# Grouped convolutions in blocks of 2 by 2 pixels instead of 4 rows by 1, values in DRAM row by row, projection out in strips of 16 rows

## The chip, the cores and the metric

The kernel runs on one core of one Trainium2 chip. The time is that of the device for one execution, in microseconds (us). A core has five engines with a queue each: PE (TensorE) multiplies matrices, and loads the stationary operand of each product first (PEld in the profile); DVE (VectorE), ACT (ScalarE) and POOL (GpSimd) work on rows of elements; SP (SyncE) issues transfers (DMAs) in order, as ACT's queue also does here. All numbers are f32.

## The reference

Two layers over `x` of 4 images, 512 channels, 64 by 64 pixels. The first is a linear attention with a second, convolved set of heads:

```python
q = h @ wq.T; k = h @ wk.T; v = h @ wv.T            # h: x with channels last
qkv = concat([q, k, v])                             # 1536 channels
dw = conv(qkv, dw_kernel, groups=3*512)             # 5 by 5, 'SAME', each channel alone
pw = conv(dw, pw_kernel, groups=3*64)               # 1 by 1, in groups of 8 channels
f = concat([qkv, pw]).reshape(B, 128, 24, N)        # 128 heads of 8, N = 4096 pixels
query, key_ = relu(f[:, :, :8]), relu(f[:, :, 8:16])
value_pad = concat([f[:, :, 16:], ones])
scores = einsum('bhdn,bhen->bhde', value_pad, key_)
out = einsum('bhde,bhen->bhdn', scores, query)
out = out[:, :, :-1] / (out[:, :, -1:] + 1e-15)
x = bn(conv1x1(out, proj_kernel)) + x
```

The second layer takes four edge maps of each channel (`sobel`, `lap`, `diag`, `grad`, from 3 by 3 neighbourhoods), multiplies each with its own 128 by 512 matrix, applies gelu, scales the channels by an attention over image means, multiplies with a 512 by 512 matrix, normalises over channels, applies gelu and adds its input.

## The kernel before

**Groups.** The outer loop runs over 16 groups: 4 images `b` times 4 groups `g` of 128 channels for each of key, value and query. A group has two phases, written out by hand as lists of steps in the order in which PE runs them: `keys_and_values` (lines 563 to 591), which also carries the rest of the group before, and `queries` (593 to 616). PE's order is that of the program text; the other engines' instructions are placed by a scheduler.

**Strips.** An image lies in 8 strips of 512 pixels, `STRIPS`: a half of the image and a number `k`. Strip `k` of a half holds every fourth row of it, 8 rows of 64 pixels. `project` (262) makes a strip of key or query with 4 products (L268). ACT copies it, and its queue writes it into `inps` with 4 DMAs (L283), where the partitions hold 4 rows of 8 channels. `values` (285) makes a strip of values with pixels in partitions: its stationary operand is `x`, 128 pixels lying side by side, its moving operand the weight (16 products of 128 columns, L290). The result `vt` goes to DRAM (`near_dram`) with 4 DMAs (L303). `turn` (313) transposes a strip of keys with 4 products whose stationary operand is the strip (L316), and `scores` (322) multiplies keys and values.

**Convolved heads.** `convolve` (394) makes 5 by 5 and 1 by 1 convolution of keys or queries in one: a block is 4 rows of 1 pixel, 32 partitions hold 4 pixels of 8 channels, and 5 column shifts times 2 blocks of rows give 10 products, each on 16 tiles of 32 by 32 of the PE array (160 products a call, L402). A call makes half an image; there are 4 calls a group, 64 in all. For values the convolution comes after the sum over pixels: `correlate` (447) multiplies the convolved keys with values of the 8 rows by 5 columns around each block, 128 by 32 stationary and 160 columns moving (L457), from patches `near` that `load_near` (434) reads back from DRAM with 4 DMAs each into 3 buffers (`VALS`). `weigh` (469) multiplies the sums with the table `wtab` of kernel weights on DVE and reduces them (L475, L476).

**Behind.** The three later stages of an image, `project_out` (618), `edge_branches` (673) and `fuse_out`, are generators whose steps run between the steps of the next image's groups (`advance`, with costs and waits in a table). `project_out` makes an output strip for 4 parts of the channels: 8 products of 512 columns from `hd` tiles (4 from `heads`, 4 from `cheads`, L643 and L645, 11 buffers), then one DVE instruction that adds a shift and `x` (L666), then a DMA into `y` (L670). `edge_branches` reads windows of rows of `y` again.

**The last image** has nothing to run behind. Its `project_out` first runs 16 of its 32 steps, which is the upper half of the image; after that its edges start, 8 rows at a time, with further steps of `project_out` and of the third image's `fuse_out` between them (`fill`):

```python
for n in range(NCH * NJ // 2):
    next(projected)
    if n in (4, 8, 12):
        next(behind[0])
```

Of the kernel before, what the change touches and what calls it, by code (L numbers as in the profile page):

```python
# [15 lines left out]
P = 128  # L16
NCH = C // P
NG = 4
# [26 lines left out]


NB = H // 4 + 1
# [5 lines left out]
DXS = (0, -2, -1, 1, 2)  # L53
VROW = 4 * 66
# [19 lines left out]
FILL_EACH = (16 * FILL_Y + 40 * FILL_F - FILL_FIRST - FILL_ATT) / (4 * NJ // 2 - 1)  # L74
# [3 lines left out]
T_PROJ, T_TURN, T_SCORES, T_CONV, T_CORR, T_SMALL = 3.4, 0.5, 0.3, 10.6, 1.1, 0.9  # L78
# [11 lines left out]
def conv_seq_kernel(  # L90
# [27 lines left out]
    def squares(ap):  # L118

        return ap.rearrange("p (b x n) -> p n x b", b=4, n=4)  # L120
# [25 lines left out]
    for t in (KEY, QUERY):  # L146
        inps[t] = keep.tile([P, 4, NB, W], F32, name=f"inp{t}")
        nc.gpsimd.memset(inps[t][:, :, 0, :], 0.0)
        nc.gpsimd.memset(inps[t][:, :, NB - 1, :], 0.0)

# [5 lines left out]

    near = [dram.tile([2, NB, W + 4, 4, 66], F32, name=f"near{n}", bufs=1) for n in range(2)]

    mixed = dram.tile([NG, P, C], F32, name="mixed", bufs=1)

    def near_border(v):

        zeros = vals.tile([P, 8 * VROW], F32, name="zeros", tag="vals")
        nc.gpsimd.memset(zeros, 0.0)
        cols = v.rearrange("a b x r d -> (a b) x (r d)")
        for at in (0, W + 2):
            nc.sync.dma_start(out=cols[:, at : at + 2, :], in_=zeros[0 : 2 * NB, 0 : 2 * VROW])
        for b, r in ((0, 0), (NB - 1, 2)):
            nc.sync.dma_start(
                out=v[:, b, :, r : r + 2, :].rearrange("a x r d -> x a (r d)"),  # L170
                in_=zeros[0 : W + 4, 0:264],
            )
# [53 lines left out]
    class Group:  # L226
# [15 lines left out]
        def load_mat(self, t):  # L242

            dp = gw.tile([P, 4, 48], F32, name="dp_sb", tag="dp_sb", bufs=2)
            nc.sync.dma_start(out=dp, in_=dpk[self.g, t // QUERY])
            self.mat[t] = gw.tile([P, 4, 40, 8], F32, name="mat", tag="mat")
            nc.gpsimd.tensor_tensor(  # L247
                self.mat[t],
                dp[:, :, 0:40].unsqueeze(3).to_broadcast([P, 4, 40, 8]),
                dp[:, :, 40:48].unsqueeze(2).to_broadcast([P, 4, 40, 8]),  # L250
# [11 lines left out]
        def project(self, t, j):  # L262
# [12 lines left out]

            r, b = (k + 2) % 4, 8 * half + (k + 2) // 4
# [5 lines left out]
            for n in range(4):  # L282
                nc.scalar.dma_start(out=inps[t][r::4, n, b : b + 8, :], in_=rows(s)[32 * n : 32 * n + 32, :, :])  # L283

        def values(self, j):
            half, k = STRIPS[j]
            ps = ps_tile("val")
            for c in range(4):
                for n in range(NCH):
                    nc.tensor.matmul(  # L290
                        ps[:, ts(c, P)], lhsT=xs[self.b, j][n][:, ts(c, P)], rhs=self.w[VALUE][:, n, :],
# [8 lines left out]
            b = 8 * half + (k + 2) // 4  # L300
            for a in range(2):
                for jp in range(2):
# [820 lines left out]
```

## Time and profile before

| | us |
|---|---|
| median of 3 runs | 5008.83 |
| lowest and highest | 4993.76, 5010.05 |
| the profiled execution's own time | 5007.84 |
| its span, first to last instruction | 5006.1 |
| busy in L268 (`project`), PE | 955.0 |
| busy in L661 (`project_out`), PE | 905.8 |
| busy in L850 (`fuse_out`), PE | 468.8 |
| busy in L738 (`edge_branches`), PE | 468.9 |
| busy in L316 (`turn`), PE | 84.3 |

The profile was taken of one execution, so sums of its parts are made against 5007.84 us. Busy time of an engine is the time in which at least one instruction of it runs; durations of single PE instructions overlap, so their mean says less than the distance of their starts. A line of a group reads: line, engine, operation, output and inputs (moving operand first, then the stationary one), shape, number, then busy time and the mean of one in ns, then the idle time ahead of it and what ended most of it. Mean granted TensorE clock is 0.972 of full speed. The 16 DMA engines are busy with queue q1 (SP) in 52.7% and with q10 (ACT) in 6.4% of the span; 627939 packets moved 864.04 MB.

### The profile page before, as it was taken

Reading aid. Unit: us, or ns where it says so; the run is one execution under the profiler, and the core shown is the slowest. Engines: PE = TensorE matmul, PEld = TensorE weight load, DVE = VectorE, ACT = ScalarE, POOL = GpSimd, SP = SyncE. Lnnn points to the kernel's source line nnn. Section 1 sums busy time; section 2 is a strip of 40 time slices with the busy share of each in tenths; the row PEclk is TensorE's granted clock in tenths of the full one; section 3 lists DMA queues with packets and bytes.
Section 4 is the critical chain, followed back from the end, with each engine's and each line's share of the span. In section 5 each row is a group of like instructions: output and inputs, shape, how many; then the busy total and the mean of one; then the engine's idle time right before and its main releaser. Section 6 shows DMA issues by size and latency. Waiting matters only on the chain. (4 is left out here: it accounts for less than half of the span.)

```text
span 5006.1 us, 106244 instructions
## 1 busy us (share of the span) xinstructions
PE 4682.3 (94%) x46140; PEld 2687.1 (54%) x46140; DVE 2099.5 (42%) x2788; ACT 1580.6 (32%) x2713; POOL 369.7 (7%) x271
## 2 busy tenths in 40 slices
PE   9999999999999999799899999989998899899897
PEld 5665654455666654354465656444446565444343
DVE  1222222114565624311356553441125565537966
ACT  2112111003454523300244443430013444304675
POOL 0000000000000012200000000220000000000343
PEclk9999999999999999899999999999999999999998
DMA  6444467675666666676556656648666565475545
GB/s 192 137 127 133 139 192 195 156 162 167 189 194 187 187 189 195 194 180 164 149 187 188 189 183 201 187 159 225 155 161 187 168 183 163 140 171 144 165 153 169
DMA packets 627939, 864.04 MB, mean 173 GB/s; under 512 B 324072, under 2 KB 381448, under 8 KB 609040
## 3 DMA queue, kind: packets, MB, share of 16 engines
q1 hardware_dynamic: 548880, 756.51, 52.7%
q10 hardware_dynamic: 78592, 100.74, 6.4%
q8 instruction: 362, 5.93, 0.5%
q14 instruction: 105, 0.86, 0.1%
HBM read 575.93 MB, written 213.98 MB: 158 GB/s over the span
## 5 line engine op out<-in xcount | busy, mean ns | idle before, releaser
L268 PE MATMUL proj<-xt,w_sb 128*128 128x512 f32 x2048 | 955.0, 610 | 55.3 <-DMA xt<-in_x 33.4
L661 PE MATMUL yps<-hd,fold_sb 128*128 128x512 f32 x2048 | 905.8, 599 | 19.5 <-DMA hd<-heads 17.4
L402 PE MATMUL cv<-inp,mat 32*32 32x512 f32 x20480 | 731.9, 597 | 40.3 <-issue 33.1
L268 PEld LDWEIGHTS proj<-xt,w_sb 128*128 128x128 f32 x2048 | 382.5, 194 | 525.5 <-issue 450.5
L661 PEld LDWEIGHTS yps<-hd,fold_sb 128*128 128x128 f32 x2048 | 386.1, 191 | 510.1 <-issue 458.2
L402 PEld LDWEIGHTS cv<-inp,mat 32*32 32x32 f32 x20480 | 422.1, 103 | 318.8 <-issue 158.2
L850 PE MATMUL zps<-ef,wf_sb 128*128 128x512 f32 (+1 forms) x1056 | 468.8, 597 | 56.5 <-DMA ef<-ef 19.0
L290 PEld LDWEIGHTS val<-w_sb,xt 128*128 128x128 f32 x4096 | 471.2, 193 | 34.5 <-issue 27.5
L290 PE MATMUL val<-w_sb,xt 128*128 128x128 f32 x4096 | 485.8, 277 | 0.6 <-DVE z L857 0.4
L738 PE MATMUL br<-maps,wbr_sb 128*128 128x256 f32 (+1 forms) x1792 | 468.9, 415 | 3.7 <-DVE s_sb L335 2.9
L666 DVE SCALAR_TENSOR_TENSOR yt<-yps,shift,xr 128x512 f32<-128x512 f32 x128 | 96.0, 750 | 837.5 <-PE yps L661 784.0
L274 ACT COPY strip<-proj 128x512 f32<-128x512 f32 x256 | 149.1, 582 | 931.0 <-PE proj L268 908.0
L738 PEld LDWEIGHTS br<-maps,wbr_sb 128*128 128x128 f32 x1792 | 338.1, 192 | 142.9 <-issue 97.1
L457 PE MATMUL corr<-near,ckt 128*32 128x160 f32 x8192 | 333.6, 315 | 35.9 <-DMA near<-near 27.5
L850 PEld LDWEIGHTS zps<-ef,wf_sb 128*128 128x128 f32 x1056 | 203.4, 196 | 299.7 <-issue 229.1
L247 POOL TENSOR_TENSOR mat<-dp_sb 128x1280 f32<-128x1280 f32 x32 | 77.5, 2421 | 3486.4 <-PE cv L402 2856.8
L457 PEld LDWEIGHTS corr<-near,ckt 128*32 128x32 f32 x8192 | 256.5, 111 | 131.9 <-issue 72.1
L714 DVE TENSOR_TENSOR maps<-dv 128x1054 f32<-128x1054 f32 (+1 forms) x112 | 158.8, 1418 | 376.5 <-PE br L738 376.3
L318 ACT ACTIVATE kt<-tr 128x512 f32<-128x512 f32 x128 | 75.8, 592 | 532.4 <-PE tr L316 350.8
L366 DVE RECIPROCAL rec<-rec 128x512 f32<-128x512 f32 x64 | 214.4, 3350 | 1.7
L746 ACT ACTIVATE ef_o<-br,shift,scale 128x256 f32<-128x256 f32 (+1 forms) x224 | 131.2, 590 | 226.8 <-PE br L738 202.8
L881 POOL TENSOR_TENSOR z<-z,yr 128x512 f32<-128x512 f32 (+1 forms) x132 | 175.9, 1351 | 293.5 <-ACT z L878 172.5
(128 smaller groups left out, 3951.8 us busy)
## 6 DMA issues: line engine op xcount, KB each, us to landing
xt<-in_x SPq DMA_DIRECT2D x316, 512.0 KB
near<-near SPq DMA_DIRECT2D x512, 264.0 KB
inp<-strip ACTq DMA_DIRECT2D x1024, 64.0 KB
win<-y SPq DMA_DIRECT2D x96, 396.0 KB
near<-vt SPq DMA_DIRECT2D x512, 66.0 KB
y<-yt SPq DMA_DIRECT2D x128, 264.0 KB
heads<-q SPq DMA_DIRECT2D x128, 256.0 KB
cheads<-cq SPq DMA_DIRECT2D x128, 256.0 KB
```

The source lines that it names most:

```text
L268: nc.tensor.matmul(ps, lhsT=self.w[t][:, c, :], rhs=xs[self.b, j][c], start=(c == 0), stop=(c == NCH - 1))
L274: nc.scalar.copy(s, ps)
L290: nc.tensor.matmul(ps[:, ts(c, P)], lhsT=xs[self.b, j][n][:, ts(c, P)], rhs=self.w[VALUE][:, n, :], start=(n == 0), stop=(n == NCH - 1),)
L366: nc.vector.reciprocal(rec, rec)
L402: nc.tensor.matmul(rows(banks[i])[32 * j : 32 * j + 32, :, c0:c1], lhsT=self.mat[t][q, j, (dx + 2) * 8 + 4 * b : (dx + 2) * 8 + 4 * b + 4, :],
L457: nc.tensor.matmul(self.banks[jj][32 * i : 32 * i + 32, 160 * b : 160 * b + 160], lhsT=self.held["c", i][:, at : at + 32], rhs=v[:, 4 * n ...
L661: nc.tensor.matmul(ps, lhsT=fold_sb[g // NG][:, g % NG, ts(c, P)], rhs=hd[g], start=(g == 0), stop=(g == 2 * NG - 1),)
L714: nc.vector.tensor_sub(flat[:, half : 3 * half - 2], dvs[:, 2 : 2 * half], dvs[:, 0 : 2 * half - 2])
L738: nc.tensor.matmul(rows(ps), lhsT=wbr_sb[:, k, c, :], rhs=rows(maps[:, slot[k], c % 2, :], WB)[:, :, 0:W], start=(c == 0), stop=(c == NCH ...
L746: nc.scalar.activation(o[:, n, :], parts[n], AF.Gelu, bias=shift1[:, k : k + 1], scale=scale1[:, k : k + 1], accum_out=pool_sb[:, k, u : u ...
L850: nc.tensor.matmul(ps, lhsT=wf_sb[:, k, ts(c, P)], rhs=ef[k], start=(k == 0), stop=(k == 3))
L881: nc.gpsimd.tensor_add(rows(z), rows(z), rows(yr, WB)[:, :, 1 : W + 1])
```

## The change

A block of the convolutions becomes 2 rows by 2 columns. A strip `k` is now one of 4 phases (row parity, column parity) of an image half, 16 rows of 32 pixels. A 5 by 5 kernel over such blocks touches 3 by 3 blocks, so `convolve` has 9 products (`BLOCKS`), with rows of 32 pixels (31 at a shifted column). A block's values come from 6 by 6 pixels; `correlate` multiplies 4 or 2 rows of 6 pixels, 192 or 96 columns. To let a partition of `near` hold blocks in a row of pixels, `values` and `turn` take every fourth pixel of a strip as their stationary operand (the new helper `every`). `near_dram` lies row by row; `values` writes it with 2 DMAs instead of 4, `load_near` reads with 2 instead of 4, in pieces of 528 floats instead of 2112. `heads` is laid out anew, and `project_out` makes strips of 16 rows (one row parity of 16 rows, so 8 rows of 64 pixels): it reads `cheads` with two DMAs per tile, `x` from two phases, and its DVE instruction puts two column phases together (`image`). The last image runs 10 steps of `project_out` ahead of its edges (`ALONE`). The planner's figures `T_CONV` and `T_CORR` are set to 9.6 and 1.0. The host lays out `x`, `dpk` and `wtab` to match; `wtab` gets smaller by a tenth, `dpk` by a twelfth.

```diff
@@ -42,16 +42,18 @@
-
-NB = H // 4 + 1
+HB, WH = H // 2, W // 2
 STRIPS = [(half, k) for half in range(2) for k in range(4)]
...
 Q_ORDER = (6, 7, 5, 4, 3, 2, 1, 0)
-DXS = (0, -2, -1, 1, 2)
-VROW = 4 * 66
+
+OUT_STRIPS = [(half, u, row) for half in range(2) for u in range(2) for row in range(2)]
+
+BLOCKS = [(dx, dy) for dx in (0, -1, 1) for dy in (0, -1, 1)]
+VROW = (W + 4) * 66
+PATCH = 4 * 8 * 66
@@ -71,11 +73,12 @@
 FILL_FIRST, FILL_ATT = 34.0, 18.0
-FILL_EACH = (16 * FILL_Y + 40 * FILL_F - FILL_FIRST - FILL_ATT) / (4 * NJ // 2 - 1)
+ALONE = 10
+FILL_EACH = ((NCH * NJ - ALONE) * FILL_Y + 40 * FILL_F - FILL_FIRST - FILL_ATT) / (4 * NJ // 2 - 1)
...
-T_PROJ, T_TURN, T_SCORES, T_CONV, T_CORR, T_SMALL = 3.4, 0.5, 0.3, 10.6, 1.1, 0.9
+T_PROJ, T_TURN, T_SCORES, T_CONV, T_CORR, T_SMALL = 3.4, 0.5, 0.3, 9.6, 1.0, 0.9
@@ -117,7 +120,11 @@
-        return ap.rearrange("p (b x n) -> p n x b", b=4, n=4)
+        return ap.rearrange("p (b r x c) -> p r c x b", b=8, r=2, c=2)
+
+    def every(ap, c):
+
+        return ap.rearrange("p (n c) -> p c n", c=4)[:, c, :]
...
@@ -154,22 +161,23 @@
-    near = [dram.tile([2, NB, W + 4, 4, 66], F32, name=f"near{n}", bufs=1) for n in range(2)]
+    near = [dram.tile([2, H + 4, W + 4, 66], F32, name=f"near{n}", bufs=1) for n in range(2)]
...
...
@@ -272,15 +280,15 @@
-
-            r, b = (k + 2) % 4, 8 * half + (k + 2) // 4
             if t == QUERY:
...
             for n in range(4):
-                nc.scalar.dma_start(out=inps[t][r::4, n, b : b + 8, :], in_=rows(s)[32 * n : 32 * n + 32, :, :])
+                nc.scalar.dma_start(
+                    out=inps[t][k::4, n, 1 + 16 * half : 17 + 16 * half, :], in_=rows(s, WH)[32 * n : 32 * n + 32, :, :]
+                )
@@ -288,7 +296,7 @@
                     nc.tensor.matmul(
-                        ps[:, ts(c, P)], lhsT=xs[self.b, j][n][:, ts(c, P)], rhs=self.w[VALUE][:, n, :],
+                        ps[:, ts(c, P)], lhsT=every(xs[self.b, j][n], c), rhs=self.w[VALUE][:, n, :],
                         start=(n == 0), stop=(n == NCH - 1),
@@ -297,15 +305,14 @@
             )
-            b = 8 * half + (k + 2) // 4
-            for a in range(2):
-                for jp in range(2):
-                    nc.sync.dma_start(
-                        out=self.near_dram[jp, b + a : b + a + 7 : 2, 2 : W + 2, (k + 2) % 4, :].rearrange(
-                            "c x d -> x c d"
-                        ),
-                        in_=vt[64 * a : 64 * a + 64, :, 2 * jp : 2 * jp + 2, :].rearrange("p c q d -> p c (q d)"),
-                    )
+            row, col = divmod(k, 2)
+            for jp in range(2):
+                nc.sync.dma_start(
+                    out=self.near_dram[
+                        jp, 2 + row + 32 * half : 2 + row + 32 * half + 32 : 2, 2 + col : 2 + col + W : 2, :
+                    ].rearrange("r (x c) d -> r x c d", c=4),
+                    in_=vt[:, :, 2 * jp : 2 * jp + 2, :].rearrange("p c q d -> p c (q d)"),
+                )
@@ -313,7 +320,7 @@
             for c in range(4):
-                nc.tensor.transpose(kt_ps[:, ts(c, P)], self.strip[j][:, ts(c, P)], ident)
+                nc.tensor.transpose(kt_ps[:, ts(c, P)], every(self.strip[j], c), ident)
             kt = work_tile("kt")
@@ -384,26 +391,30 @@
             for k in range(4):
-                j = 4 * half + k
                 q = work_tile("q")
-                nc.vector.tensor_mul(q, self.rq.pop(j), banks[k])
-                nc.sync.dma_start(out=self.heads[j, :, self.g, :], in_=q)
+                nc.vector.tensor_mul(q, self.rq.pop(4 * half + k), banks[k])
+                row, col = divmod(k, 2)
+                nc.sync.dma_start(
+                    out=self.heads[half, :, row, :, self.g, col, :].rearrange("u p x -> p u x"),
+                    in_=q.rearrange("p (u x) -> p u x", u=2),
+                )
...
             banks = quad_tiles("cv")
-            last = len(DXS) * 2 - 1
-            for n, (dx, b) in enumerate((dx, b) for dx in DXS for b in range(2)):
-                c0, c1 = _span(dx, W)
+            for n, (dx, dy) in enumerate(BLOCKS):
+                c0, c1 = _span(dx, WH)
+                at = 4 * (3 * (dx + 1) + dy + 1)
+                r0 = 1 + 16 * half + dy
                 for j in range(4):
...
                         nc.tensor.matmul(
-                            rows(banks[i])[32 * j : 32 * j + 32, :, c0:c1],
-                            lhsT=self.mat[t][q, j, (dx + 2) * 8 + 4 * b : (dx + 2) * 8 + 4 * b + 4, :],
-                            rhs=inps[t][q, j, 8 * half + b : 8 * half + b + 8, c0 + dx : c1 + dx],
-                            start=(n == 0), stop=(n == last),
+                            rows(banks[i], WH)[32 * j : 32 * j + 32, :, c0:c1],
+                            lhsT=self.mat[t][q, j, at : at + 4, :],
+                            rhs=inps[t][q, j, r0 : r0 + 16, c0 + dx : c1 + dx],
+                            start=(n == 0), stop=(n == len(BLOCKS) - 1),
                         )
@@ -411,11 +422,10 @@
                         self.ksum = mini.tile([P, 4, 4], F32, name="ksum")
-                    for a in range(2):
+                    for r in range(2):
                         nc.scalar.activation(
-                            o.rearrange("p (n a x b) -> p a n x b", n=4, a=2, b=4)[:, a],
-                            squares(banks[i][:, 256 * a : 256 * a + 256]), AF.Relu,
-                            accum_out=self.ksum[:, 2 * half + a, i : i + 1],
+                            o.rearrange("p (r c x b) -> p r c x b", r=2, c=2, b=8)[:, r], squares(banks[i])[:, r],
+                            AF.Relu, accum_out=self.ksum[:, 2 * half + r, i : i + 1],
                         )
@@ -436,28 +446,33 @@
                 if half is not None:
-                    self.near[at] = vals.tile([P, 8 * VROW], F32, name="near", tag="vals")
-                    for part in range(4):
-                        v = self.near_dram[jp, 8 * half + b + 4 * (part // 2), 32 * (part % 2)]
+                    self.near[at] = vals.tile([P, PATCH], F32, name="near", tag="vals")
+                    for part in range(2):
+                        v = self.near_dram[jp, 4 * (8 * half + b), 32 * part]
                         nc.sync.dma_start(
-                            out=self.near[at][32 * part : 32 * part + 32, :],
-                            in_=bass.AP(v.tensor, v.offset, [[4 * VROW, 8], [(W + 4) * VROW, 4], [1, 8 * VROW]]),
+                            out=self.near[at][64 * part : 64 * part + 64, :],
+                            in_=bass.AP(v.tensor, v.offset, [[4 * 66, 8], [VROW, 32], [1, 8 * 66]]),
                         )
...
                 self.banks = [psum.tile([P, 512], F32, tag="quad", name="corr") for _ in range(2)]
-            b = step // 2
-            v = self.near[half, jp, b].rearrange("p (x d) -> p x d", d=66)
-            for n in range(2 * (step % 2), 2 * (step % 2) + 2):
+            b, r = step // 2, step % 2
+            v = self.near[half, jp, b].rearrange("p (r x d) -> p r x d", r=4, x=8)
+
+
+            r0, r1 = (2 * r, 4) if b == 0 else (0, 2 + 2 * r)
+            w0 = 4 * b + r0 - 2 * r
+            for n in (2 * r, 2 * r + 1):
+                c0 = 2 * (n % 2)
                 for jj in range(2):
...
                         nc.tensor.matmul(
-                            self.banks[jj][32 * i : 32 * i + 32, 160 * b : 160 * b + 160],
+                            self.banks[jj][32 * i : 32 * i + 32, 48 * w0 : 48 * (w0 + r1 - r0)],
                             lhsT=self.held["c", i][:, at : at + 32],
-                            rhs=v[:, 4 * n : 4 * n + 20, 33 * jj + 8 * i : 33 * jj + 8 * i + 8],
+                            rhs=v[:, r0:r1, c0 : c0 + 6, 33 * jj + 8 * i : 33 * jj + 8 * i + 8],
                             start=(b == 0 and n == 0), stop=(b == 1 and n == 3),
@@ -471,14 +486,14 @@
             for n in range(2):
-                w = work_tile("weighed", 320)
-                nc.vector.tensor_mul(w, self.banks[n][:, 0:320], self.wtab[:, 2 * jp + n, :])
+                w = work_tile("weighed", 288)
+                nc.vector.tensor_mul(w, self.banks[n][:, 0:288], self.wtab[:, 2 * jp + n, :])
                 nc.vector.tensor_reduce(
...
         def load_wtab(self):
-            self.wtab = gw.tile([P, 4, 320], F32, name="wtab_sb", tag="wtab_sb", bufs=1)
+            self.wtab = gw.tile([P, 4, 288], F32, name="wtab_sb", tag="wtab_sb", bufs=1)
             nc.sync.dma_start(out=self.wtab, in_=wtab[self.g])
@@ -634,28 +649,38 @@
-            def load(j):
-                half, k = STRIPS[j]
+            def load(half, u, row):
                 hd = []
...
                     if g < NG:
-                        nc.sync.dma_start(out=t, in_=heads[j, :, g, :])
+                        nc.sync.dma_start(out=t, in_=heads[half, u, row, :, g].rearrange("p c x -> p (c x)"))
                     else:
-                        nc.sync.dma_start(
-                            out=t,
-                            in_=cheads[half, g - NG].rearrange("i (j m e) x -> m (i j) e x", j=4, m=4)[3 - k],
-                        )
+                        for col in range(2):
+                            nc.sync.dma_start(
+                                out=t[:, ts(col, 256)],
+                                in_=cheads[half, g - NG].rearrange("i (j m e) x -> m (i j) e x", j=4, m=4)[
+                                    2 * row + col, :, :, ts(u, 256)
+                                ],
+                            )
                     hd.append(t)
...
-            for j, (half, k) in enumerate(STRIPS):
-                hd = load(j)
-                if j == 0:
+            def image(ap):
+
+                return ap.rearrange("p (c r x) -> p r x c", c=2, r=8)
+
+            for n, (half, u, row) in enumerate(OUT_STRIPS):
+                hd = load(half, u, row)
+                if n == 0:
                     yield WAIT_Y
...
                     xr = pool.tile([P, 512], F32, name="xr", tag="xr", bufs=3)
-                    nc.sync.dma_start(out=xr, in_=x[b, j, :, c, :])
+                    j = 4 * half + 2 * row
+                    nc.sync.dma_start(
+                        out=xr.rearrange("p (c x) -> p c x", c=2),
+                        in_=x[b, j : j + 2, :, c, 256 * u : 256 * u + 256].rearrange("c p x -> p c x"),
+                    )
                     ps = ps_tile("yps")
@@ -664,10 +689,11 @@
                     nc.vector.scalar_tensor_tensor(
-                        yt[:, :, 1 : W + 1], rows(ps), shift0[:, c : c + 1], rows(xr), ALU.add, ALU.add
+                        yt[:, :, 1 : W + 1].rearrange("p r (x c) -> p r x c", c=2), image(ps),
+                        shift0[:, c : c + 1], image(xr), ALU.add, ALU.add,
                     )
-                    at = 1 + k + 32 * half
-                    nc.sync.dma_start(out=y[c, :, at : at + 29 : 4, :], in_=yt)
+                    at = 1 + row + 16 * (2 * half + u)
+                    nc.sync.dma_start(out=y[c, :, at : at + 15 : 2, :], in_=yt)
                     yield SHARE_Y / (NJ * NCH)
...
@@ -996,9 +1022,9 @@
     next(behind[0])
-    for n in range(NCH * NJ // 2):
+    for n in range(ALONE):
         next(projected)
-        if n in (4, 8, 12):
+        if n in (3, 6, 9):
             next(behind[0])
...
```

## The prediction

> **What bounds the kernel now.** I read the engine rows and the slices first, then PE's waits, then the groups by line, and last the timeline of a stretch in which one call of each product can be timed from start to start.
>
> ```profile
> span 5006.1 us, 106244 instructions
> PE 4682.3 (94%) x46140; PEld 2687.1 (54%) x46140; DVE 2099.5 (42%) x2788; ACT 1580.6 (32%) x2713; POOL 369.7 (7%) x271
> PE   9999999999999999799899999989998899899897
> DMA  6444467675666666676556656648666565475545
> ```
>
> PE is busy in 94% of the span and in nearly every slice; DVE, ACT, POOL and the DMA engines have room. 324 us of PE idleness are left, and PE's own waits show how they are scattered:
>
> ```profile
> PE proj L268 <- DMA xt<-in_x: 33.4, 4, 18.0
> PE cv L402 <- issue: 33.1, 26, 3.4
> PE corr L457 <- DMA near<-near: 27.5, 7, 8.5
> ```
>
> The columns are the sum, the number and the longest. No wait is large; the waits on DMA that this list names add up to about 100 us. So an edit is worth what it does to PE's time, almost one to one. The groups concerned:
>
> ```profile
> L402 PE MATMUL cv<-inp,mat 32*32 32x512 f32 x20480 | 731.9, 597 | 40.3 <-issue 33.1
> L290 PEld LDWEIGHTS val<-w_sb,xt 128*128 128x128 f32 x4096 | 471.2, 193 | 34.5 <-issue 27.5
> L290 PE MATMUL val<-w_sb,xt 128*128 128x128 f32 x4096 | 485.8, 277 | 0.6 <-DVE z L857 0.4
> L457 PE MATMUL corr<-near,ckt 128*32 128x160 f32 x8192 | 333.6, 315 | 35.9 <-DMA near<-near 27.5
> ```
>
> Each product of the program is two instructions here (f32), each with its own weight load. Means of one overlap; a cost is read from starts:
>
> ```profile
> 4109.11 0.46 PE L327 MATMUL s<-vt,kt 128*32 128x33 f32 x32
> 4109.50 0.66 PE L316 MATMUL tr<-consts_sb,strip 128*128 128x128 f32 x4
> 4109.99 3.74 PE L290 MATMUL val<-w_sb,xt 128*128 128x128 f32 x32
> 4113.57 3.62 PE L738 MATMUL br<-maps,wbr_sb 128*128 128x256 f32 x16
> 4117.12 10.65 PE L402 MATMUL cv<-inp,mat 32*32 32x512 f32 x320
> 4127.70 3.70 PE L268 MATMUL proj<-xt,w_sb 128*128 128x512 f32 x8
> ...
> 4204.07 2.54 PE L457 MATMUL corr<-near,ckt 128*32 128x160 f32 x64
> 4206.54 1.13 PE L356 MATMUL fold<-p,stt 128*128 128x512 f32 x2
> ```
>
> One convolution takes 10.58 us; `values` 3.58 us, 112 ns for each of 32 pairs of load and matmul; `turn` 0.49 us, 122 ns for each of 4; `scores` 0.39 us, 49 ns for a group of four column tiles of 33 columns; a correlation 154 ns for a group of four with 160 columns.
>
> [...] In `values` both sides are thus of equal length, and a longer load shows at once. [...] The trace of before has no weight load with a stride, but DVE shows the effect:
>
> ```profile
> L476 DVE TENSOR_REDUCE ct<-weighed 128x8 f32<-128x320 f32 x128 | 88.3, 727 | 0.1
> L475 DVE TENSOR_TENSOR weighed<-corr,wtab_sb 128x320 f32<-128x320 f32 x128 | 57.3, 484 | 195.7 <-PE corr L457 187.0 <-DMA near<-vt 8.0 <-DMA near<-near 0.7
> L806 DVE TENSOR_REDUCE wf_mean<-wf_sb 128x4 f32<-128x2048 f32 x4 | 9.1, 2283 | 24.6 <-DMA wf_sb<-in_wfuse 24.6
> ```
>
> The reduction of 320 values, read at a step of 8 floats, takes 243 ns more than the multiplication of 320 lying side by side, 0.76 ns per value; a reduction in itself is not slow (2048 neighbours in 2283 ns). About 1.8 ns per value instead of 1.04.
>
> **The change part by part.**
>
> Convolutions: 10 products become 9. Mean columns stay (before 2 of 512, 4 of 504, 4 of 496, mean 502; after 3 of 512 and 6 of 496, mean 501), and so do the 32 load-matmul pairs of each. A tenth of 731.9 us goes: -73 us. The moving rows become 16 of 31 instead of 8 of 62; [...]counted as nothing (at worst a few us).
>
> Correlations: the number of products stays, 8192 instructions in 2048 groups of four, but half have 192 columns and half 96 instead of 160. From 49 ns at 33 columns and 154 at 160, a column costs 0.83 ns and a group 22 ns. So 181 and 101 ns, mean 141 against 154: 13.3 ns x 2048 = -27 us. If short groups hit a floor of 154 ns it would be +28 us; the 49 ns of `scores` exclude that. Runs of 8 floats in the moving operand are as before.
>
> `values` and `turn`: their stationary operands become `every(..., c)`, columns at a step of 4 floats, 16 bytes[...]. 4096 loads in `values`, 512 in `turn`. From below: nothing, if the weight path doesn't mind. From above: DVE's figure as it stands, 1.8 ns x 128 = 230 ns. I take twice the present time[...]: +107 ns, beside which DVE's excess of 0.76 ns x 128 = 97 ns stands. `values` gets 219 ns per pair: 4096 x 107 = +438 us. `turn`: from 122 to 219 ns, 512 x 97 = +49 us. Both are on PE in order, with nothing on PE that could run in their place; only DMA waits behind them get shorter, at most a part of the 100 us named: I take -15 us.
>
> Transfers: writing patches takes 2 issues for 4 and reading them 2 for 4, with 2112 bytes in a piece instead of 8448; `heads` writes, `cheads` reads and `xr` go in pieces of 1 KB for 2 KB, with 128 more issues for `cheads`. SP's issues fall by 384 in all. New packets: 49152 for patches and 16384 each for the other three, 98304. A packet of queue q1 costs 77 ns in the mean (52.7% of 16 x 5006 us over 548880), so at most 98304 x 77 / 16 = 473 us of the 16 engines, 9 points on a mean of 59%; from below nothing, as bytes stay. The cover is PE's work ahead of three patch buffers and eleven `hd` tiles; without it the 100 us of DMA waits would grow by a sixth, 15 us. Counted at 0 to +15. `cheads` now has two DMAs behind one wait for a free `hd` tile; behind it on SP stand the `xr` and `y` transfers, 0.5 us each, covered by 7 us of PE per output tile.
>
> DVE's addition in `project_out` reads `ps` and `xr` with a step of 256 floats inside: 0 to 0.76 ns x 512 = 0.39 us on 750 ns, 128 times. It hides under PE's 7 us per tile (DVE waits 784 us for PE there), except in the last batch; at worst +10 us. ACT's convolution copies keep their step in PSUM. The product of `mat` on POOL shrinks by a tenth, hidden.
>
> End: strips of 16 rows let the last batch's edges begin after 10 output tiles instead of 16, 6 x 6.9 = 41 us earlier, so that DVE's work spreads.
>
> ```profile
> 4700.00:4800.00 100.00, 82.77 (x185) 35.96 (x184) 97.13 (x63) 70.05 (x83) 47.99 (x25) 0.91 0.47 150
> ```
>
> In this stretch (PE, PEld, DVE, ACT, POOL) DVE is full and PE idles 17 us, which is what can come back: -15 us, bounds -30 and +10 (the strided addition). What is late next is the chain of the final pieces, which stays.
>
> Sum: -73 - 27 + 438 + 49 - 15 - 15 = +357 us on the profiled execution's own 5007.84 us (its span is 5006.1), which lies 1 us below the median of the runs: 5365 us; I write 5360, no finer than the terms are.
>
> **Rivals.** (A) The stride costs the weight path nothing. Then -73 - 27 - 15 = -115, of which DMA waits, now less covered, give back some 15 to 30: about 4915 us, 4885 to 4955. [...] Against it: DVE's 0.76 ns. The point from which the sign turns: 115 us over 4608 loads, 25 ns per load. (B) A penalty just there, 15 to 30 ns: no change, 4990 to 5025. (C) DMA takes PE's place: smaller packets make patches late, with rival A's loads. Even the whole 9 points only raise the mean share to 68%, so it would be 4990 at most; I count it within A and B.
>
> **How the numbers follow.** About 0.3% of a time can't be told from no change here. Doubled loads or nearly so (70 to 125 ns more): 0.77, own range 5200 to 5475: 4608 x 70 = 323 less 115 gives 5216 and 4608 x 123 = 567 less 115 gives 5460, with 15 us of DMA waits either way. Rival A 0.20, rival B and C 0.03. Leaving A out would leave out more than two in ten together with the slow case's own edges, so the range reaches to A: 4900 to 5475.
>
> **What would show it.** Right: `values` takes about 7 us from start to start instead of 3.58, its PEld row near 300 ns for 193 and PEld's total near 3150 us; `turn` near 0.9 us; a convolution 9.5 us; correlations alternate between 181 and 101 ns a group; PE still over 93%. Wrong: `values` at 3.6 us, then the time falls below 4960. Wrong in another way: PE's share drops below 90% with waits on `near` or `hd`.

## The result, and the profile after

| | us | ratio to before, 95% interval |
|---|---|---|
| before, median of the 4 runs of that comparison | 5006.35 (4993.76 to 5010.05) | |
| after, median of 4 | 5558.35 (5553.42 to 5560.44) | 1.1106 [1.1085, 1.1128] |

The change makes the kernel slower by 552 us; 357 were forecast. The profiled execution of after took 5560.44 us, its span is 5558.7. First the engine rows and slices of after:

```profile
span 5558.7 us, 101767 instructions
...
PE 5121.5 (92%) x44092; PEld 3141.0 (57%) x44092; DVE 2086.8 (38%) x2788; ACT 1590.9 (29%) x2718; POOL 350.3 (6%) x271
...
PE   9999999899897989979979998999987989889987
...
PEclk9999999999998999989989999999998999999998
```

PE works 439 us longer than before (4682.3), and it idles 437 us instead of 324, in holes all over the span. So there are two losses, one inside PE's work and one between. The groups tell of the first (the last line of this view, and the same line of before under it, are the loads of `turn`):

```profile
L298 PEld LDWEIGHTS val<-w_sb,xt 128*128 128x128 f32 x4096 | 967.2, 329 | 30.8 <-issue 20.5
L298 PE MATMUL val<-w_sb,xt 128*128 128x128 f32 x4096 | 977.7, 397 | 0.0
L413 PE MATMUL cv<-inp,mat 32*32 32x512 f32 x18432 | 667.1, 603 | 50.4 <-issue 43.1
...
L323 PEld LDWEIGHTS tr<-consts_sb,strip 128*128 128x128 f32 x512 | 72.1, 209 | 7.8 <-issue 2.7 <-DVE s_sb L342 0.4
```

```profile
L316 PEld LDWEIGHTS tr<-consts_sb,strip 128*128 128x128 f32 x512 | 54.8, 141 | 11.0 <-issue 5.4 <-ACT lap L720 0.3 <-ACT ef_o L746 0.3
```

`values` has doubled (485.8 before): +492. The convolution's products lost 65 (731.9), the correlation's 23 (333.6 to 311.0), `turn` grew by 11 (84.3 to 95.4). PE's timeline has the same from start to start:

```profile
1523.55 7.74 PE L298 MATMUL val<-w_sb,xt 128*128 128x128 f32 x32
1531.21 1.14 PE L388 MATMUL over<-rec,consts_sb 32*128 32x512 f32 x8
...
1583.66 0.75 PE L323 MATMUL tr<-consts_sb,strip 128*128 128x128 f32 x4
1584.24 3.62 PE L764 MATMUL br<-maps,wbr_sb 128*128 128x256 f32 x16
1587.79 9.64 PE L413 MATMUL cv<-inp,mat 32*32 32x512 f32 x288
1597.36 3.72 PE L764 MATMUL br<-maps,wbr_sb 128*128 128x256 f32 x16
```

7.66 us for `values`, 0.58 for `turn`, 9.57 for a convolution. The second loss stands in PE's waits (sum, number, longest), first after, then before:

```profile
PE corr L472 <- DMA near<-near: 57.0, 15, 7.3
PE ctr L439 <- ACT ckt L441: 55.4, 11, 29.3
PE ctr L439 <- ACT co L426: 52.2, 5, 26.4
```

```profile
PE corr L457 <- DMA near<-near: 27.5, 7, 8.5
...
PE ctr L429 <- ACT ckt L431: 14.6, 11, 4.0
...
PE ctr L429 <- ACT co L415: 8.4, 3, 4.8
```

`ctr` are the products that transpose the convolved keys. ACT is busy for 29% only, so a wait of 26 or 29 us for one of its copies says that something held ACT up. The timeline of its queue, SP's and PE's around 2440 us shows what (a line joins several issues, with the time from the first to the end of the last):

```profile
2405.97 11.01 SPq L660 DMA_DIRECT2D hd<-cheads  x8
...
2426.46 10.85 SPq L657 DMA_DIRECT2D hd<-heads  x3
...
2419.54 18.49 ACTq L289 DMA_DIRECT2D inp<-strip  x4
2438.13 1.56 ACT L441 COPY ckt<-ctr 128x512 f32<-128x512 f32 x3 [30.42 <-DMA inp<-strip]
...
2438.77 1.11 PE L439 MATMUL ctr<-consts_sb,co 128*128 128x128 f32 x4 [29.35 <-ACT ckt L441]
```

Four issues on ACT's queue, 18.49 us from the first to the end of the last, stand ahead of a copy that PE needs; SP's issues come slowly as well. ACT's four issues themselves took 0.48 to 0.54 us each. The rest is waiting, and the semaphores in the trace say for what: all transfers of SP and ACT mark their landing on eight semaphores in turn, and nine issues in ten (3234 of 3585 in after) wait until the transfer that had their semaphore last, in either queue, has landed. ACT's second issue started at 2430.46, when a patch read that SP had issued at 2417.73 had landed at 2430.09; the third and the fourth started when two reads of `x` of SP had landed. So a late transfer of SP holds up ACT. ACT's waits of this kind over 0.3 us add up to 197 us in after and to 83 us in before.

In the windows table this stretch has PE at 2.12 of 31 us, a granted clock of 0.61, and the DMA engines busy:

```profile
2407.00:2438.00 31.00, 2.12 (x17) 0.81 (x15) 4.04 (x2) 0.71 (x2) 0.00 (x0) 0.61 0.84 226
```

The last two numbers are the share of the 16 DMA engines (0.84) and GB/s. The tail gained: PE's waits at `zps` for ACT's `z` went from 17.2 to 5.7 us, and in the last 500 us PE idles 44 us instead of 56.

### The profile page after: what moved, and what is told of

It reads as the page before. It is cut to its first block, busy times and chain, and to the rows that moved or that the text cites. A ratio compares the mean times of both kernels' runs of the same rounds, so it can differ in the third digit from the quotient of the medians.

```text
span 5558.7 us, 101767 instructions
## 1 busy us (share of the span) xinstructions
PE 5121.5 (92%) x44092; PEld 3141.0 (57%) x44092; DVE 2086.8 (38%) x2788; ACT 1590.9 (29%) x2718; POOL 350.3 (6%) x271
## 3 DMA queue, kind: packets, MB, share of 16 engines
q1 hardware_dynamic: 644080, 755.19, 52.5%
## 5 line engine op out<-in xcount | busy, mean ns | idle before, releaser
L276 PE MATMUL proj<-xt,w_sb 128*128 128x512 f32 x2048 | 970.7, 618 | 67.9 <-DMA xt<-in_x 34.9
L298 PEld LDWEIGHTS val<-w_sb,xt 128*128 128x128 f32 x4096 | 967.2, 329 | 30.8 <-issue 20.5
L298 PE MATMUL val<-w_sb,xt 128*128 128x128 f32 x4096 | 977.7, 397 | 0.0
L413 PE MATMUL cv<-inp,mat 32*32 32x512 f32 x18432 | 667.1, 603 | 50.4 <-issue 43.1
L413 PEld LDWEIGHTS cv<-inp,mat 32*32 32x32 f32 x18432 | 385.6, 104 | 299.9 <-issue 152.9
L472 PE MATMUL corr<-near,ckt 128*32 128x192 f32 (+1 forms) x8192 | 311.0, 306 | 58.9 <-DMA near<-near 57.0
L305 DVE COPY vt<-val 128x512 f32<-128x512 f32 x128 | 88.5, 692 | 679.7 <-PE val L298 674.3
L255 POOL TENSOR_TENSOR mat<-dp_sb 128x1152 f32<-128x1152 f32 x32 | 70.6, 2207 | 3950.9 <-PE cv L413 3101.2
L472 PEld LDWEIGHTS corr<-near,ckt 128*32 128x32 f32 x8192 | 222.4, 113 | 168.5 <-issue 88.4
```

The lines of the kernel that those rows point to most:

```text
L276: nc.tensor.matmul(ps, lhsT=self.w[t][:, c, :], rhs=xs[self.b, j][c], start=(c == 0), stop=(c == NCH - 1))
L298: nc.tensor.matmul(ps[:, ts(c, P)], lhsT=every(xs[self.b, j][n], c), rhs=self.w[VALUE][:, n, :], start=(n == 0), stop=(n == NCH - 1),)
L413: nc.tensor.matmul(rows(banks[i], WH)[32 * j : 32 * j + 32, :, c0:c1], lhsT=self.mat[t][q, j, at : at + 4, :], rhs=inps[t][q, j, r0 : r0 + ...
L472: nc.tensor.matmul(self.banks[jj][32 * i : 32 * i + 32, 48 * w0 : 48 * (w0 + r1 - r0)], lhsT=self.held["c", i][:, at : at + 32], rhs=v[:, ...
```

## Experiments

All were timed beside the kernel before, whose median is 4979 to 5006 us in the five sets; so a difference between two sets is good to some 27 us. "Plain" means after with both stationary operands lying side by side.

| kernel | us | ratio, interval | PE busy |
|---|---|---|---|
| before, both operands strided | 5454.42 | 1.0916 [1.0897, 1.0934] | 5160.6 |
| after, `values` side by side | 5121.16 | 1.0249 [1.0224, 1.0274] | 4642.0 |
| plain | 5102.88 | 1.0224 [1.0203, 1.0245] | 4627.6 |
| plain, patches as before (32 partitions, 8448 B) | 4895.56 | 0.9783 [0.9765, 0.9800] | 4580.0 |
| before, after's patch reads (64 partitions, 2112 B) | 5128.34 | 1.0243 [1.0210, 1.0276] | 4712.8 |
| plain, patches by one DMA (128 partitions) | 5024.13 | 1.0047 [1.0030, 1.0064] | 4635.9 |
| plain, 2 KB pieces for `heads`, `cheads`, `x` | 5110.76 | 1.0215 [1.0189, 1.0240] | |
| plain, 32 partitions, 2112 B | 4890.30 | 0.9778 [0.9748, 0.9808] | 4570.5 |
| plain, 64 partitions, 8448 B | 5097.65 | 1.0187 [1.0159, 1.0216] | 4637.2 |
| after, 32 partitions, 2112 B | 5364.09 | 1.0724 [1.0699, 1.0750] | 5068.3 |

The plain kernels keep `values`' two writes per strip, so the values land at other pixels, which alters the data and no amount of work; the same holds of the two edits to the kernel before. Whole kernels with side-by-side loads come in the last part.

### The stride alone

Theory at this point: the stride is the whole loss of PE's work; what else is late is a second effect. The kernel before got the stride and nothing else; after lost it in `values`, then in both.

```diff
-  ps[:, ts(c, P)], lhsT=xs[self.b, j][n][:, ts(c, P)], rhs=...
+  ps[:, ts(c, P)], lhsT=every(xs[self.b, j][n], c), rhs=...
-  nc.tensor.transpose(kt_ps[:, ts(c, P)], self.strip[j][:, ts(c, P)], ident)
+  nc.tensor.transpose(kt_ps[:, ts(c, P)], every(self.strip[j], c), ident)
```

Before with both of these edits:

> The kernel before with one edit: values and turn take every fourth pixel as their stationary operand (the keys and values then go with other pixels than their places say). Stride theory: PE busy 4682 + 492 + 11 = 5185 us. With idle time as before, about 5510 us; if the longer phases also make PE wait, up to 5620 us. If a stride costs something only together with the new transfers, it stays near 5006.

After with the first undone:

> The changed kernel with one edit: the stationary operand of the products in values is again 128 pixels lying side by side (the values then stand for other pixels than their places say). Stride theory: a load at a step of 16 bytes takes about 236 ns instead of 112, so values falls from 978 to about 486 us of PE and PE's busy time from 5121 to about 4630. What the idle time of PE (437 us) does tells two theories of its growth by 113 us apart. If it comes from the new pieces of the transfers, it stays: about 5066 us. If it comes from the longer values phases, which shift when transfers meet, it falls to the 324 us of before: about 4955 us. If the stride is not the cause, values stays near 978 us and the time near 5558.

After with both undone:

> As e1_values_plain, and the stationary operand of turn is side by side too (keys and values then agree in their pixels, but the patches in DRAM still have the other order). Turn should fall from 95 to 84 us, so 11 us below e1_values_plain: about 5055 us if the transfers make the idle time, about 4945 if the long phases do. The forecast had counted 49 us for turn; if the busy time hid the rest of it, the time falls by up to 49 us instead.

Measured 5454.42, 5121.16 and 5102.88 us. The stride by itself costs the kernel before 457 us (5454.42 less 4997.33), with the same group line as in after:

```profile
L294 PEld LDWEIGHTS val<-w_sb,xt 128*128 128x128 f32 x4096 | 967.2, 329 | 29.9 <-issue 21.6 <-DVE maps L721 1.1 <-DVE s_sb L339 0.8
```

That a stride makes loads longer is thus shown (967.2 us busy in place of 471.2, 193 to 329 ns in the mean); other steps, 8 bytes for one, were not run, so why it does is not. `turn` is worth at most 18 us (5121.16 less 5102.88; the runs of the two overlap). But the plain kernel should have been below before by the 115 us that the prediction counts for fewer products, waits and tail, and is 105 above: some 220 us were still unexplained.

### Patch reads: the first guess, and why it fell

The plain kernel then got the patch reads of before (four DMAs, pieces of 8448 bytes; it reads bytes that are not these patches), and before got those of after.

```diff
-  for part in range(2):
-      v = self.near_dram[jp, 4 * (8 * half + b), 32 * part]
+  for part in range(4):
+      v = self.near_dram[jp, 8 * half + b + 4 * (part // 2), 32 * (part % 2)]
...
-      out=self.near[at][64 * part : 64 * part + 64, :],
-      in_=bass.AP(v.tensor, v.offset, [[4 * 66, 8], [VROW, 32], [1, 8 * 66]]),
+      out=self.near[at][32 * part : 32 * part + 32, :],
+      in_=bass.AP(v.tensor, v.offset, [[4 * 264, 8], [68 * 264, 4], [1, 8 * 264]]),
```

> e2_both_plain with the patches read as in the kernel before, 4 DMAs of 32 pieces of 8448 bytes on 8 engines (the patches then hold other pixels). Patch theory, if the size of the pieces is what jams: about 4980 us, and the waits of corr on near fall from 56 to about 28 us. 1 KB theory and order theory: about 5100.

The reverse, in before:

> The kernel before with the changed kernel's reads of patches alone: 2 DMAs of 256 pieces of 2112 bytes instead of 4 of 32 pieces of 8448 (the patches then hold other pixels). Patch theory: PE idles about 100 us more, 5100 us instead of 4997. 1 KB theory and order theory: 4997, within 15 us.

The traces don't say which engine moves a piece. What they show for the 8 engines of the expectations is the number of pieces under way: in before exactly 8 of patches in 64% of the time in which any is, and more in 4%; in after, with other transfers of 2112 bytes among them, 8 or 9 in 54%.

4895.56 and 5128.34 us: the patch reads are worth 207 us in one kernel and 127 in the other, without any other edit. This edit changes two things at once, the size of a piece and the number of partitions of a transfer. The smaller pieces of `heads`, `cheads` and `x` were ruled out as the cause by giving them 2 KB again (one DMA per tile, whole rows; other rows are read):

> e2_both_plain with pieces of 2 KB again in heads, cheads and xr, and one DMA for a tile of cheads instead of two (project_out then mixes pixels wrongly). 1 KB theory: the idle time goes back to that of before, about 4960 to 4990 us. Patch theory: at most the 24 us that yps waits for cheads and some of xt's, about 5075. Order theory: about 5100.

5110.76, no gain on 5102.88. Next, each buffer was read by one DMA of 128 partitions, with an outer dimension of 16, in place of two with 8; on how many engines it runs was not shown:

```diff
-  in_=bass.AP(v.tensor, v.offset, [[4 * 66, 8], [VROW, 32], [1, 8 * 66]]),   # twice, 64 partitions
+  in_=bass.AP(v.tensor, v.offset, [[4 * 66, 16], [VROW, 32], [1, 8 * 66]]),  # once, 128
```

> e2_both_plain with a patch read by one DMA whose outermost dimension is 16 instead of two whose outermost is 8 (same pieces of 2112 bytes[...]; the patches still have another order of pixels than the keys). Patch theory (the patches' small pieces jam eight of the engines and so make PE wait): the idle time of PE falls from 471 us to some 350, the time from 5103 to about 4980. Theory of the 1 KB pieces (heads, cheads, xr): nothing changes, about 5100. Theory of the order (neither, but where the planner puts steps): about 5100.

5024.13: 79 of the 207 us. Up to here it looked as if small pieces were the cause. So I laid the values out in blocks of 4 rows, which makes a patch one piece of 8448 bytes again, with the whole computation in place (values written by 8 DMAs of 32 partitions per strip); by rows with 8 writes was run as its base:

```diff
-  near = [dram.tile([2, H + 4, W + 4, 66], ...
+  near = [dram.tile([2, H // 4 + 1, W + 4, 4, 66], ...
...
-  in_=bass.AP(v.tensor, v.offset, [[4 * 66, 8], [VROW, 32], [1, 8 * 66]]),
+  in_=bass.AP(v.tensor, v.offset, [[16 * 66, 8], [4 * VROW, 8], [1, PATCH]]),
...
```

By rows, 8 writes:

> The changed kernel with both stationary operands side by side and the patches written to match, a strip of values by 8 DMAs of 32 partitions instead of 2 of 128 (same pieces of 264 bytes). PE as e2_both_plain, about 4618 us busy. 768 more issues on SP at 0.6 us are 460 us on a queue that issues for 1324 us now: if they hide, 5055 us (transfers make the idle time) or 4945 us (long phases do); if SP gets late with them, up to 5200 us.

In blocks:

> Both stationary operands side by side, and the values lie in DRAM in blocks of 4 rows, so that a patch of 6 by 6 is one piece of 8448 bytes again (2 transfers of 64 pieces); the values are written by 8 transfers of 32 partitions per strip in place of 2. Theory (stride and small pieces are the whole loss, the fewer products are worth their 105 us): PE busy near the 4580 us of the version with large pieces, and a time between that version's 4896 us and 4980 us, the higher end if the six more issues per strip cost what they cost in the version that wrote by rows (80 us). Rival (the version with large pieces was fast only because its reads did not follow the values they are computed from): 5080 to 5120 us, as with small pieces.

5183.05 us by rows and 5188.58 in blocks. Pieces four times as large brought nothing. The time in blocks lies outside of what either theory gave as its range; with 80 us for the eight writes (5183.05 less 5102.88) the rival's would hold it, so it was still open whether reading the right bytes had to be slow. Counted over the packets of the traces, a piece of 8448 bytes takes 376 ns in the mean in before and 370 in the plain kernel that reads as before, but 551 ns in blocks. What differs is the destination: transfers of 32 partitions there, of 64 here.

### Partitions of a transfer

A median piece of 8448 bytes takes 319 ns in before, 26.5 GB/s. Theory P below says that the number of partitions of a transfer is what makes pieces longer, 64 against 32; theory S says that it is their size.

Size and number of partitions were confounded so far. Two kernels separate them, and a third puts reads of 32 partitions into the changed kernel as it is:

```diff
-  for part in range(2):
-      v = self.near_dram[jp, 4 * (8 * half + b), 32 * part]
+  for part in range(4):
+      v = self.near_dram[jp, 4 * (8 * half + b) + 16 * (part // 2), 32 * (part % 2)]
...
-      out=self.near[at][64 * part : 64 * part + 64, :],
-      in_=bass.AP(v.tensor, v.offset, [[4 * 66, 8], [VROW, 32], [1, 8 * 66]]),
+      out=self.near[at][32 * part : 32 * part + 32, :],
+      in_=bass.AP(v.tensor, v.offset, [[4 * 66, 8], [VROW, 16], [1, 8 * 66]]),
...
-  for r in range(2):
-      nc.scalar.activation(o.rearrange("p (r c x b) -> p r c x b", r=2, c=2, b=8)[:, r], ...
+  for r in range(2):
+      for v in range(2):
+          nc.scalar.activation(o.rearrange("p (r c v x b) -> p r v c x b", r=2, c=2, v=2, b=4)[:, r, v], ...
```

Small pieces, 32 partitions:

> Both stationary operands side by side, values row by row, patch reads in pieces of 2112 bytes as in the change, but in four transfers of 32 partitions in place of two of 64[...]. The order of the pixels over partitions is changed with it, and ScalarE writes the convolved key in four operations per tile in place of two. Theory P ([...]the size of the pieces costs little): 4880 to 4940 us, waits for patches at the correlation down to 25 us as with large pieces, a patch's pieces down from 141 to about 90 to 100 ns each. Theory S (the size of the pieces is the loss): 5080 to 5120 us, as the version with both operands side by side.

Large pieces, 64 partitions:

> The version with large pieces (8448 bytes, which took 4896 us) with two transfers of 64 partitions in place of four of 32; the reads fetch other bytes than the values' patches, so the correlations are of other data. Theory P: 5050 to 5120 us, pieces up from 370 to about 550 ns, waits at the correlation about 55 us. Theory S: 4896 us within 20.

The changed kernel, small pieces, 32 partitions:

> The changed kernel, every fourth column loaded as it has it, with only the patch reads in four transfers of 32 partitions (and the pixels' order and ScalarE's four operations that go with it). Theory P, effects add: 5558 less the 207 us that large pieces on 32 partitions took off, 5330 to 5400 us. Theory S: 5540 to 5570 us.

4890.30, 5097.65 and 5364.09 us: between 32 and 64 partitions per transfer it is their number that decides, and the size of the pieces doesn't. The third kernel reads the right bytes, so the reads were not fast only where they fetched other ones. Large pieces on 64 partitions take 523 ns instead of 370; packets of 2112 bytes (four fifths of them patch pieces) go from 139 ns in the plain kernel to 105, median 120 to 86. Of the large pieces on 32 partitions 84% take 300 to 350 ns, on 64 only 21% do, and the next commonest stretch is 600 to 650 (19%), twice 319. So a part of the pieces takes twice as long; why was not shown. A transfer of 64 partitions also has twice the bytes to land for one semaphore (528 KB against 264), and no kernel took the same 64 partitions in another order. One transfer of 128 lies between the two (5024.13 us), so more partitions are not slower in every case.

How do longer pieces make PE wait? SP's own issues of the patch reads (ns, min/median/max), first in after, then in the plain kernel with 32 partitions:

```profile
L452 SPq DMA_DIRECT2D near<-near x256: 569/608/6576, 58.7 to 4827.9; - x128
```

```profile
L454 SPq DMA_DIRECT2D near<-near x512: 675/676/1341, 49.4 to 4153.4; - x171
```

The long issues are gone in the latter kernel, and so are PE's waits for ACT:

```profile
PE corr L474 <- DMA near<-near: 28.5, 10, 5.2
...
PE ctr L441 <- ACT ckt L443: 11.4, 11, 1.9
```

But large pieces on 64 partitions have all the waits, though none of their patch issues is long:

```profile
L452 SPq DMA_DIRECT2D near<-near x256: 567/584/1346, 51.0 to 4371.9; - x128
```

```profile
PE corr L472 <- DMA near<-near: 56.5, 16, 7.2
PE ctr L439 <- ACT ckt L441: 54.5, 10, 30.4
```

So it isn't the length of these issues that PE's waits come from. What goes with them is ACT's waiting for shared semaphores: 373 us in this kernel and 265 in the plain one, against 89, 71 and 50 in the three with 32 partitions (plain with large pieces, plain with small ones, after).

### A kernel with the gain and without the losses

Side-by-side loads put the pixels otherwise over the partitions, so a whole kernel needs 8 writes of values per strip in place of 2. In blocks I had tried one patch read of 128 partitions in place of two of 64, and, with two of 64, POOL as the issuer of these writes:

> As the version in blocks of 4 rows, but each patch buffer read by one transfer whose outer dimension is 16[...]. Theory that the number of engines counts besides the size of the pieces: 20 to 60 us below the version with 8 engines, 4850 to 4930 us. Rival (the wait of PE for its own issue at the convolution, which grew from 45 to 133 us[...]): no gain or a loss, the wait for issue above 100 us again.

> As the version in blocks of 4 rows, but the 8 writes of values per strip are issued by POOL instead of SP. If SP's issues are what the 8 writes cost: 20 to 60 us below that version, down to the 4896 us of the version with large pieces. If the small writes of 264 bytes themselves load the engines: no change within 10 us. If POOL's own work stands behind a blocked issue: slower, with waits for POOL at the products of query and key.

5031.87 and 5059.82 us, ratios 1.0101 [1.0069, 1.0132] and 1.0161 [1.0133, 1.0190]: better than 5188.58 by 157 and 129 us, not better than before. With patch reads of 32 partitions, by rows, first SP and then POOL issuing:

```diff
+  for r in range(4):
+      for jp in range(2):
+          at = 2 + row + 32 * half + 2 * r
+          nc.gpsimd.dma_start(                  # nc.sync in the first
+              out=self.near_dram[jp, at : at + 25 : 8, 2 + col : 2 + col + W : 2, :].rearrange("c x d -> x c d"),
+              in_=vt[32 * r : 32 * r + 32, :, 2 * jp : 2 * jp + 2, :].rearrange("p c q d -> p c (q d)"),
```

> A whole kernel without either loss: both stationary operands side by side, patch reads in four transfers of 32 partitions, and the values, whose pixels then lie otherwise over the partitions, written by 8 transfers of 32 partitions per strip in place of 2. The same with patch reads on 64 partitions took 5183 us, 80 above the version with 2 writes. If the two effects add: 4890 + 80 = 4970 us, 4940 to 4990, just under the kernel before. If the writes cost only because SP was held up by the patch reads: 4890 to 4920 us.

> As that version, with the 8 writes of values issued by POOL in place of SP. In blocks of 4 rows and with 64-partition reads POOL took 129 us off. If SP's issues are what the writes cost, 4870 to 4910 us, under both kernels by 2 per cent; if the writes on POOL were only better because SP was held up, as the version on SP within 15 us.

4973.62 us, 0.9984 [0.9975, 0.9994], and 4881.81 us, 0.9794 [0.9768, 0.9820]. The writes cost 83 us on SP (4973.62 less 4890.30, from two sets; 103 by the ratios to before) with 32 partitions, and 80 with 64, so the two effects roughly add. Issued by POOL, otherwise busy for 7% (351.7 us in the plain kernel with 32 partitions), the writes cost 92 us less than on SP. Why was not separated: POOL's transfers also go through a queue of their own (q0, 34.67 MB) and move in packets of 2112 bytes where SP's take 264. This kernel computes the whole reference and is 2.1% faster than the kernel before (1.8 to 2.3). Its engine row, and the group of its writes on POOL:

```profile
PE 4582.6 (94%) x44092; PEld 2615.0 (53%) x44092; DVE 2078.5 (42%) x2788; ACT 1627.7 (33%) x3232; POOL 905.4 (19%) x1295
```

```profile
L312 POOL DMA_DIRECT2D near<-vt x1024 | 555.3, 550 | 1853.8 <-DVE vt L305 1322.0 <-DVE csb L553 179.2 <-DVE s_sb L344 120.7
```

## Why the prediction was right and wrong

The direction and the larger cause, the loads with a stride, were right; the size was 195 us short, and 5558 lies outside of 4900 to 5475.

- **The step that failed** is the one on transfers: "2112 bytes in a piece instead of 8448", "The cover is PE's work ahead of three patch buffers and eleven `hd` tiles; without it the 100 us of DMA waits would grow by a sixth, 15 us. Counted at 0 to +15", and rival C's bound, "Even the whole 9 points only raise the mean share to 68%, so it would be 4990 at most; I count it within A and B". It counted packets and bytes, and a mean share of the engines. With it fell "an edit is worth what it does to PE's time, almost one to one": PE's idle time grew by 113 us. The change from 32 to 64 partitions per transfer stood in the diff and was read only as fewer issues. It costs 194 us in the changed kernel (5558.35 less 5364.09) and 213 in the plain one (5102.88 less 4890.30, from two sets). The mean share of queue q1 didn't even rise (52.7 to 52.5%, of a longer span); the loss lies in stretches in which the engines are busy (0.84 of them around 2420 us, 0.28 in before at that time) and transfers land late, so that the next issues wait for their semaphores, and ACT's computing waits behind them in ACT's own queue. Three buffers cover a late patch (its waits grew by 30 us only), but not an issue that waits ahead of other work. The plain kernel is rival C as it was written, late patches with loads that cost nothing more: 5103 us against its bound of 4990.
- **`values`**: forecast +438 us (107 ns a pair), measured +492, 120 ns. The 107 was a guess that no trace gave; measured in before were a pair's 112 ns and DVE's 0.76 ns a value, 97 for 128. That the loads lengthen, to about twice, holds; the bound from above was too low, 230 ns per 128 columns from DVE's reduction against 239 busy per pair. That DVE's row gave about the right size is luck: its addition in `project_out`, whose neighbours now lie 1 KB apart, took no longer (754 ns, 750 before), so DVE's time with one step is no sure measure for a load.
- **`turn`**: forecast +49, measured +11. Its loads grew from 141 to 209 ns in the mean, those of `values` from 193 to 329. Why a transpose's load loses less was not tried.
- **Convolutions and correlations**: forecast -73 and -27. In after -65 and -23; in the changed kernel with 32 partitions 658.7 and 300.0 us, so -73 and -34. That PE runs slower after stalls (below) fits the difference.
- **Rest**: the tail gave about 12 of its 15 us, and the bound of +10 for DVE's addition wasn't needed. The DMA waits' -15 was overrun by the patch reads; in the changed kernel with 32 partitions PE idles 287 us, 37 less than before, where 30 were counted for waits and tail.
- **The sum** of everything but the 64 partitions was right: 5364.09 us where 5365 was worked out. That it fits to 1 us is luck, since `values` (+54 off) and `turn` (-38) offset each other. Rival A's price, 4915 us with 4885 to 4955 around it, is what the plain kernels with 32 partitions took (4890, 4896); its premise, a stride for nothing, was false.

## What to carry to other kernels

Of a transfer that changes shape, look at the number of partitions that it writes, not only at its bytes, packets and issues: here 64 partitions in place of 32 cost 194 and 213 us in two kernels, and why was not shown. A stationary operand with its columns 16 bytes apart cost as much again as the load itself (239 ns a pair instead of 119), in products whose loads had been busy as long as they were (471.2 us of 485.8). A DMA issue in the queue of an engine that also computes held up the work behind it: a copy of ACT stood behind four issues that took 18.49 us from the first to the end of the last, and PE waited 29.35 us for it. So when an engine with low busy time is waited for, look at what the issues in its queue wait for, a transfer of another queue among them.

## What was not expected of the hardware

- **PE after a stall.** The same 4 products of `project` (8 instructions) that take 3.6 to 3.7 us in the 200 us ahead took 6.77 after 8 us of idleness, in after's timeline, at a granted clock of 0.54 where the call ahead (3.70 us, at 1699.65) had 1.00:

```profile
1718.08 6.77 PE L276 MATMUL proj<-xt,w_sb 128*128 128x512 f32 x8 [8.32 <-DVE s_sb L342]
```

  If this is the rule after a hole, holes are dearer than they are long. It fits that between the plain kernel with 64 partitions and that with 32, busy time fell by 57 us (4627.6 to 4570.5) with the same 44092 PE instructions, and the mean clock rose from 0.955 to 0.975.
- **Patch reads by one DMA of 128 partitions** cut the waits for patches, from 56.0 us in the plain kernel, but PE's waits for its own issue at the convolution rose, from 45.2 us in the plain kernel:

```profile
PE cv L413 <- issue: 133.2, 53, 4.8
...
PE corr L471 <- DMA near<-near: 13.0, 5, 4.7
```

  In blocks of 4 rows it was 119.8 us, so it goes with the one DMA per buffer and not with the size of the pieces. What it is was not settled.
- **A late transfer holds up both queues**: patch reads go through SP alone, yet ACT waited for them, since the program's eight semaphores are shared. In after, 94 of ACT's 197 us were waits for the landing of a patch read. A kernel with semaphores for each queue alone was not run.
